# Half B of a recurrent step: which product is made from bf16 parts, how its x term arrives, and how the x work is dealt out over eight steps

## The chip, the cores and the metric

The kernel runs on one core of one Trainium2 chip. The metric is the device time of one execution in microseconds (us). Before the change it is 1639.37 us, the median of three runs (1638.94 to 1640.77).

## The reference

A gated recurrence runs over 512 time steps for a batch of 8, with 512 inputs and 512 hidden units, everything in float32:

```python
fused = jax.nn.sigmoid(jnp.concatenate([x_t, h], axis=-1) @ w_W + w_b)
hidden_state, output_state = jnp.split(fused, 2, axis=-1)
memory_state = x_t @ wx_W + wx_b + hidden_state * (h @ wh_W + wh_b)
h_new = output_state * h + (1.0 - output_state) * jnp.tanh(memory_state)
```

The output is x plus the stacked h_new. In the kernel's names r is the pre-activation of hidden_state, z that of output_state, and hh is h @ wh_W + wh_b. All products with x can be made ahead of time; the products with h can't, since step i+1 needs h of step i.

## The kernel before

**Layout.** The hidden units are cut into half A and half B. TensorE holds h of four chunks of 128 units (k = 0 to 3; chunks 0 and 1 come out of half A, 2 and 3 out of half B) as the stationary operand, 32 columns wide, and streams weights past it; four column tiles j of 32 columns work side by side. Four steps make a group, and a group's x terms (bias included) are spread into the PSUM banks ahead of the h products, in rows of 8 batches for each step of the group.

**A step on TensorE** follows the string `ORDER`: bank A (192 columns: hh, z and r of half A) for the four chunks, bank B (128 columns: r and hh of half B), then bank C (64 columns: z of half B, in the PSUM tile `cs`), then `x_step`, a share of the x products for a later pair of groups. A0 and B0 stand first, since chunk 0 of the new h is there first; A2 and A3 need half B of the new h.

**Bank C is made in two ways.** In float32 every product is one instruction in the program, two loads and two matmuls in the trace. From step 24 on, in every second group (steps 0 to 3 of eight, `in_parts`), it is made from bf16 parts: POOL splits h into three bf16 parts (`split`), and for each chunk and column tile one load of 24 columns (3 parts x 8 batches) serves three matmuls with three bf16 parts of the weights (`wb`, `w2`, `w3`; `kept` is a matmul that keeps the loaded operand). The three row groups of the result are added by a VectorE reduction (`tzs<-tzB`).

**The chain of a step.** VectorE transposes r, hh and z of half A out of bank A, ScalarE takes the sigmoid of r, a scan on VectorE makes r * hh + x (slots of two elements, `md0`, `md1`), ScalarE takes the tanh, and another scan makes the new h (`hT<-hd0A,hT`). It is done in two pieces for each half (`memory(hf, q)`, `update(hf, q)`). Half B follows in the same way from banks B and C.

**The x work.** `x_step` deals 2688 columns over eight steps u = 0 to 7 by the table `SHARE`. The sums end up in the SBUF tiles `even` and `odd` (even and odd groups), half by ScalarE copies and half by VectorE additions: `even[HI, XC]` is written at the end of step u = 5, `odd[LO, XC]` at the end of u = 7. `spread` copies them into banks A and B, `spread_c` into the four cells of `cs` with a mask for each step (in the other groups bank C is one copy), and `turn_x` transposes the columns of wx into `md1`.

**Queues.** The program is one list of operations in the order in which they are written; each engine takes its own in that order, and a planner puts in the waits. PSUM is guarded by bank: an access waits for the last access of any other engine to that bank. SyncE (SP) issues the loads of x (one of 64 KB at u = 1 and u = 5) and the stores of the output (one at the end of u = 3 and of u = 7).

## Time and profile before

| | us |
|---|---|
| median of three runs | 1639.37 |
| the profiled execution: its own time | 1637.59 |
| the profiled execution: span of its core | 1635.5 |
| TensorE matmul busy | 1625.4 (99%) |
| TensorE loads busy | 1397.4 (85%) |
| ScalarE busy | 1254.0 (77%) |
| VectorE busy | 1235.8 (76%) |
| GpSimd (POOL) busy | 531.8 (33%) |

The granted TensorE clock is 1.0 throughout. A busy matmul row isn't an engine at its peak, since matmuls overlap in the trace; what a step costs is read from the distance between the starts of its first matmul and that of the next step. In the rows PE is a matmul, PEld a load of the stationary operand, DVE VectorE, ACT ScalarE and SPq SyncE's DMA queue. The columns of a timeline are start (us from the span's start), length, engine, line, operation, output<-inputs, shape and count, and in brackets the idle time before it with its releaser. Nearly all rows have line 255, that of a helper that emits the program.

### The profile page before, as it was taken

To read this page: it belongs to the slowest core of one execution; us is meant where nothing else is said; L and a number is where in the kernel's file an instruction comes from. 1 tells how busy PE (TensorE), PEld (TensorE's weight loads), DVE (VectorE), ACT (ScalarE), POOL (GpSimd) and SP (SyncE) were. 2 spreads that over 40 slices of the span, in tenths; PEclk is the share of its full clock that TensorE was granted. 3 is DMA by queue.
4 is the path that set the end of the run, shared out by engine and by line. 5 is a ranking of instruction groups with operands and counts; after the bars stand their busy time and mean duration, and the time that the engine had idled before them with its cause. 6 is when DMAs were issued, how large, how long until landed. Compare 5 with 4: busy or idle time off the path is not lost.

```text
span 1635.5 us, 127307 instructions
## 1 busy us (share of the span) xinstructions
PE 1625.4 (99%) x58202; PEld 1397.4 (85%) x50394; DVE 1235.8 (76%) x9433; ACT 1254.0 (77%) x6188; POOL 531.8 (33%) x2272
## 2 busy tenths in 40 slices
PE   8999999999999999999999999999999999999998
PEld 5988898988888888888888888888888888988887
DVE  7777777777777777777777777777777777777776
ACT  4777777778777777777777777777777777777775
POOL 1323323333233333332333333323333333333332
PEclk9999999999999999999999999999999999999999
DMA  4000000000000000000000000000000000000000
GB/s 185 12 14 18 15 15 14 18 15 14 15 18 15 15 14 18 15 15 15 17 15 15 15 18 14 15 15 18 14 15 15 17 15 15 15 18 10 10 10 11
DMA packets 37297, 31.25 MB, mean 19 GB/s; under 512 B 4084, under 2 KB 35060, under 8 KB 36600
## 3 DMA queue, kind: packets, MB, share of 16 engines
q1 hardware_dynamic: 36576, 22.89, 4.5%
q8 instruction: 425, 6.96, 1.7%
q14 instruction: 144, 1.18, 0.2%
q10 hardware_dynamic: 152, 0.22, 0.0%
HBM read 14.70 MB, written 8.39 MB: 14 GB/s over the span
## 4 chain that ended last, share of the span: by engine, by line
PE 98%; DVE 1%; DMA 0%; ACT 0%; issue 0%; DVEq 0%; ACTq 0%; SPq 0%
PE A L255 41%; PE B L255 27%; PE xp L255 17%; PE cs L255 9%; PE cs L219 4%; PE eps L255 1%; DMA head<-in_xh_dram 0%; DVE tr L255 0%; DVE m L255 0%; DVE tw L255 0%; DVE hT L255 0%; DVE md1A L255 0%; DVE tz L255 0%; DVE md1B L255 0%; DVE even L255 0%
## 5 line engine op out<-in xcount | busy, mean ns | idle before, releaser
L255 PE MATMUL A<-wa,hT 128*32 128x192 f32 x16384 | 872.3, 327 | 3.2 <-DVE hT L255 3.1
L255 PEld LDWEIGHTS A<-wa,hT 128*32 128x32 f32 x16384 | 549.4, 122 | 189.8 <-DVE hT L255 132.1
L255 PE MATMUL B<-wb,hT 128*32 128x128 f32 x16384 | 652.0, 273 | 0.0
L255 PEld LDWEIGHTS B<-wb,hT 128*32 128x32 f32 x16384 | 542.5, 122 | 19.9 <-DMA wb<-in_wb_dram 0.3
L255 POOL TENSOR_TENSOR ot<-xin,hT 128x16 f32<-128x16 f32 x991 | 224.1, 250 | 598.8 <-DVE hT L255 596.8
L255 ACT ACTIVATE hT<-m 128x8 f32<-128x8 f32 x2048 | 349.2, 208 | 65.0 <-DVE m L255 64.1
L255 DVE STREAM_TRANSPOSE tr<-A 128x64 f32<-128x64 f32 x512 | 127.9, 250 | 291.9 <-PE A L255 285.8
L255 PE MATMUL xp<-tw,sx 128*32 128x384 f32 (+2 forms) x1464 | 264.0, 433 | 0.0
L255 POOL TENSOR_TENSOR split<-hT 128x32 f32<-128x32 f32 x488 | 126.0, 258 | 410.0 <-DVE m L255 397.9
L255 ACT ACTIVATE hT<-hT 128x16 f32<-128x16 f32 x1022 | 210.3, 225 | 50.1 <-DVE hT L255 47.8
L255 ACT ACTIVATE md0A<-tr 128x16 f32<-128x16 f32 x512 | 112.2, 219 | 165.4 <-DVE tr L255 158.8
L255 DVE TENSOR_TENSOR_SCAN hT<-hd0B,hT 128x24 f32<-128x24 f32 x1024 | 179.5, 204 | 75.7 <-ACT hT L255 52.4
L255 PE MATMUL xp<-wx,xin 128*32 128x384 f32 (+4 forms) x1348 | 218.3, 413 | 0.0
L255 DVE TENSOR_TENSOR_SCAN hT<-hd0A,hT 128x24 f32<-128x24 f32 x1024 | 198.3, 194 | 0.0
L255 PE MATMUL cs<-wb,hT 128*32 128x64 f32 x8576 | 173.0, 219 | 0.0
L255 PEld LDWEIGHTS cs<-wb,hT 128*32 128x32 f32 x8576 | 161.4, 122 | 0.0
L255 DVE TENSOR_TENSOR_SCAN m<-md0A,md1A 128x16 f32<-128x16 f32 x1024 | 142.3, 181 | 6.9
L255 DVE TENSOR_TENSOR_SCAN m<-md0B,md1B 128x16 f32<-128x16 f32 x1024 | 145.0, 163 | 0.6 <-issue 0.4
L255 ACT ACTIVATE hd0A<-tz 128x16 f32<-128x16 f32 x512 | 116.0, 227 | 20.9
L219 PE MATMUL cs<-w,split 128*24 128x64 bf16 x7808 | 129.9, 192 | 0.0
L255 PE MATMUL cs<-wb,split 128*24 128x64 bf16 x3904 | 122.2, 192 | 0.0
L255 POOL TENSOR_TENSOR split<-split 128x16 f32<-128x16 f32 x488 | 105.2, 216 | 38.2
(101 smaller groups left out, 2216.0 us busy)
## 6 DMA issues: line engine op xcount, KB each, us to landing
out_dram<-ot SPq DMA_DIRECT2D x128, 64.0 KB, 1.6
xin<-in_x_dram SPq DMA_DIRECT2D x112, 64.0 KB, 2.4
wx<-in_wx_dram SPq DMA_DIRECT2D x4, 768.0 KB, 7.5
wa<-in_wa_dram SPq DMA_DIRECT2D x4, 384.0 KB, 10.1
wb<-in_wb_dram SPq DMA_DIRECT2D x1, 1152.0 KB, 13.4
xin<-in_x_dram SPq DMA_DIRECT2D x3, 256.0 KB, 3.1
wb<-in_wb_dram SPq DMA_DIRECT2D x1, 384.0 KB, 13.8
head<-in_xh_dram ACTq DMA_DIRECT2D x1, 208.0 KB, 5.6
```

The costliest lines, as they stand in the source:

```text
L219: return t.add_instruction(mybir.InstMatmult(name=self.nc.get_next_instruction_name(), ins=[t.lower_ap(rhs), t.lower_ap(lhsT)], outs=[t.lo ...
L255: inst = getattr(self, item.op, getattr(engine, item.op, None))(*item.args, **item.kw)
```

## The change

1. **What is made from parts.** The third product of half B is now hh (`H` in `ORDER`) in place of z; r and z of half B come from bank B. It is made from bf16 parts in every step from 24 on (`in_parts`), into one of eight cells of `cs`. Before step 24 the same cells are filled in float32.
2. **Slots of four rows.** `split` has four rows for each batch: three parts and a row of zeros. So the 32 rows of a column tile in a cell are 8 batches x 4. The fourth row of the cell holds the x term, the first one the bias of hh. A scan over four elements for each batch (`md0B` holds 0 or 1, 1, 1, r; `memB` is the transposed cell) adds the three parts, multiplies by r and adds the x term, so the reduction and half B's `turn_x` go.
3. **The x term travels by DMA.** `move_x` issues 16 DMAs for each group, of 8 partitions x 64 columns each, from `even` or `odd` into the fourth rows of `xz`, one for each step of the group and each column tile. `fill` copies one step of `xz` into its cell on ScalarE, two steps ahead, in every step; `spread_c` and the copies into bank C go.
4. **Shares of the x work.** `SHARE` becomes 306, 384, 384, 384, 308, 306, 308, 308 for u = 0 to 7 (it was 384 four times and 288 four times). The sum stays 2688.
5. POOL splits h in every step from 24 on, not in half of them; before that it copies h into the split tile.

The core of the diff:

```diff
-ORDER = "A0 B0 A1 A2 A3 B1 B2 B3 C0 C1 C2 C3"
+ORDER = "A0 B0 A1 A2 A3 B1 B2 B3 H0 H1 H2 H3"
...
-SHARE = [384, 384, 384, 384, 288, 288, 288, 288]
+SHARE = [306, 384, 384, 384, 308, 306, 308, 308]
...
-XP = {"A": slice(0, 192), "X": slice(192, 320), "C": slice(320, 384), "B": slice(384, 512)}
+XP = {"A": slice(0, 192), "X": slice(192, 256), "M": slice(256, 320), "B": slice(320, 448)}
...
+    def products_h(i, k):
+
+        four = split[i % 2]
+        for j in range(NQ):
+            to = cell(i)[32 * j : 32 * j + 32]
+            if not in_parts(i):
+                mm(to, four[:, k].rearrange("p b u -> p (b u)"), wh("H", k, j))
+                continue
+            lhsT = high(four)[:, k].rearrange("p b u -> p (b u)")[:, 1::2]
+            for n, t_ in enumerate((wh("H", k, j), w2[:, k, j], w3[:, k, j])):
+                (nc.tensor.kept if n else mm)(to, lhsT, high(t_)[:, 1::2])
...
     def in_parts(i):
-        return 3 * NH <= i < T and i // GS % 2 == 0
+        return 3 * NH <= i < T
...
+    def move_x(g):
+
+        at = (even, odd)[g % 2]
+        if source(g) is not at:
+            nc.scalar.copy(at[:, XP["M"]], source(g)[:, XP["M"]])
+        for s in range(GS):
+            for j in range(NQ):
+                r = 32 * j
+                (nc.sync if g or s else nc.scalar).dma_start(
+                    out=xz[g % 2][r + 3 : r + 32 : 4, s],
+                    in_=at[r + B * s : r + B * s + B, XP["M"]],
+                )
+
+    def fill(i):
+        if i < T:
+            nc.scalar.copy(cell(i), xz[i // GS % 2][:, i % GS])
...
-            "h": (pa[:, :HU], ps["B"][:, HU:]),
-            "z": (pa[:, HU : 2 * HU], cell(i)),
-            "r": (pa[:, 2 * HU :], ps["B"][:, :HU]),
+            "h": (pa[:, :HU], cell(i)),
+            "z": (pa[:, HU : 2 * HU], ps["B"][:, :HU]),
+            "r": (pa[:, 2 * HU :], ps["B"][:, HU:]),
...
-            scan(c_, ms[hf], md0[hf][g % 2][:, rows], md1[hf][g % 2][:, rows])
-            act(state(hf, i, 1)[:, :, c_], ms[hf][:, :, c_, 1], AF.Tanh)
+            d1 = memB.rearrange("p c (n s) -> p n c s", s=4) if hf else md1[g % 2][:, rows]
+            scan(c_, ms[hf], md0[hf][g % 2][:, rows], d1)
+            act(state(hf, i, 1)[:, :, c_], ms[hf][:, :, c_, SL[hf] - 1], AF.Tanh)
...
         turn_r(1)
+        turn_z(1)
+        update(0, 0)
         turn_h(1)
-        update(0, 0)
...
+        for n in (1, 2) if i == 0 else () if i == T - 6 else (i + 1, i + 2) if i == T - 5 else (i + 2,):
+            fill(n)
...
         elif u == 5:
             if sums:
                 nc.vector.tensor_tensor(even[HI, XC], reg(BE), both[HI], ALU.add)
+            if sums or o + 1 == LAST:
+                move_x(2 * o + 2)
...
             if o:
                 nc.scalar.copy(odd[LO, XC], reg(GA))
-            turn_x(2 * o + 2, 1)
+            if sums:
+                move_x(2 * o + 3)
```

How the change moves instructions is shown on three engines. First VectorE, from the transposes of half B to the last update in a step that was made from parts before (`tr` is r, `md1B` hh, `tzB` the three row groups of z, `m` the scan of the memory state, `hT` the new h). Before:

```order
L255 STREAM_TRANSPOSE tr_1_136<-B_117 128x64 [waits flow_tensor]
L255 STREAM_TRANSPOSE md1B_86<-B_117 128x64
L255 SCALAR_TENSOR_TENSOR hT_69<-hd0A_89,hT_68 128x24 [waits flow_scalar]
L255 STREAM_TRANSPOSE tzB_156<-cs 128x64 [waits flow_tensor]
L255 SCALAR_TENSOR_TENSOR m_1_133<-md0B_82,md1B_86 128x16 [waits flow_vector,flow_scalar]
L255 TENSOR_REDUCE tzs_157<-tzB_156 128x16 [waits flow_vector]
L255 SCALAR_TENSOR_TENSOR hT_69<-hd0A_89,hT_68 128x24
L255 SCALAR_TENSOR_TENSOR m_1_133<-md0B_82,md1B_86 128x16
L255 SCALAR_TENSOR_TENSOR hT_69<-hd0B_91,hT_68 128x24 [waits flow_scalar] x2
```

The same place after the change, in a step u = 5 (`memB` is the transposed cell of hh):

```order
L257 STREAM_TRANSPOSE tr_1_138<-B_119 128x64 [waits flow_tensor]
L257 STREAM_TRANSPOSE tz_1_139<-B_119 128x64
L257 SCALAR_TENSOR_TENSOR hT_73<-hd0A_89,hT_72 128x24 [waits flow_scalar]
L257 STREAM_TRANSPOSE memB_133<-cs 128x64 [waits flow_tensor]
L257 SCALAR_TENSOR_TENSOR hT_73<-hd0A_89,hT_72 128x24 [waits flow_scalar]
L257 SCALAR_TENSOR_TENSOR m_1_135<-md0B_85,memB_133 128x32 [waits flow_vector]
L257 SCALAR_TENSOR_TENSOR m_1_135<-md0B_85,memB_133 128x32
L257 SCALAR_TENSOR_TENSOR hT_73<-hd0B_91,hT_72 128x24 [waits flow_scalar] x2
```

The reduction is gone, the scans of half B take 32 elements, and the first of them waits for VectorE's own transpose of the cell, two instructions ahead of it. The first update of half A stands at the same place.

Second ScalarE, from the last tanh of a step u = 6 to the first sigmoid of the next step (`cs<-...` fills a cell, `hT<-hT` copies the new h into another slot, A and B are banks). Before:

```order
L255 ACTIVATE hT_73<-m_2_140 128x8 [waits flow_vector] x2
L255 ACTIVATE cs<-even,mask 128x64 x2
L255 ACTIVATE hT_74<-hT_74 128x8x2
L255 ACTIVATE hT_74<-hT_74 128x8x2 [waits flow_vector]
L255 COPY A_116<-even 128x192
L255 COPY B_117<-even 128x128
L255 ACTIVATE md0A_81<-tr_3_148 128x2x8 [waits flow_vector]
```

After:

```order
L257 ACTIVATE hT_73<-m_2_143 128x8 [waits flow_vector] x2
L257 COPY cs<-xz_80 128x64 [waits flow_dma13,flow_dma14,flow_dma12,flow_dma11]
L257 ACTIVATE hT_74<-hT_74 128x8x2
L257 ACTIVATE hT_74<-hT_74 128x8x2 [waits flow_vector]
L257 COPY A_116<-even 128x192
L257 COPY B_117<-even 128x128
L257 ACTIVATE md0A_83<-tr_3_152 128x2x8 [waits flow_vector]
```

One copy stands where two masked copies stood, and it waits for four DMAs. A copy like it now stands in every step.

Third SyncE's queue. Before, eight steps hold two stores and two loads in turn, and only the stores wait (for POOL's sums). After, from a store at the end of u = 3 to the next store at the end of u = 7:

```order
L257 DMA out_dram<-ot_158 128x128 [waits flow_gpsimd]
L257 DMA xin_132<-in_x_dram 128x128
L257 DMA xz_80<-even 8x64 x2
L257 DMA xz_80<-even 8x64 [waits flow_vector]
L257 DMA xz_80<-even 8x64 x13
L257 DMA xz_81<-odd 8x64 [waits flow_scalar]
L257 DMA xz_81<-odd 8x64 x3
L257 DMA xz_81<-odd 8x64 [waits flow_dma19]
L257 DMA xz_81<-odd 8x64 [waits flow_dma20]
L257 DMA xz_81<-odd 8x64 [waits flow_dma21]
L257 DMA xz_81<-odd 8x64 [waits flow_dma22]
L257 DMA xz_81<-odd 8x64 x8
```

There are 32 more DMAs in eight steps, between one store and the next. The first two of the even group read partitions that ScalarE wrote at u = 2; the third waits for the VectorE addition of u = 5.

177 lines of the change are left out of this document (83 added, 94 removed).

## The prediction

> **What bounds the kernel now.** I read the page's busy times and its chain that ended last, then the waits, then the timeline of TensorE over two kinds of steps. A change of less than 0.2% (3.3 us) is what a measurement of this kernel can't tell from no change.
>
> ```profile
> PE 1625.4 (99%) x58202; PEld 1397.4 (85%) x50394; DVE 1235.8 (76%) x9433; ACT 1254.0 (77%) x6188; POOL 531.8 (33%) x2272
> PE 98%; DVE 1%; DMA 0%; ACT 0%; issue 0%; DVEq 0%; ACTq 0%; SPq 0%
> PEld A L255 <- DVE hT L255: 132.1, 402, 0.8
> PE A L255 <- DVE hT L255: 3.1, 9, 0.6
> ```
>
> Matmuls make 98% of the chain, and TensorE waits for the new h only 9 times. But the load for bank A waits for it 402 times, so the loop through h ends just ahead of the matmuls. How far ahead is read step by step:
>
> ```profile
> 797.64 0.52 PE L255 MATMUL A<-wa,hT 128*32 128x192 f32 x8
> ...
> 799.82 0.64 PE L255 MATMUL cs<-wb,hT 128*32 128x64 f32 x32
> 800.26 0.42 PE L255 MATMUL xp<-wx,xin 128*32 128x288 f32 x2
> ...
> 800.68 0.22 PEld L255 LDWEIGHTS A<-wa,hT 128*32 128x32 f32 x8 [0.28 <-DVE hT L255]
> ...
> 800.75 0.52 PE L255 MATMUL A<-wa,hT 128*32 128x192 f32 x8
> ...
> 802.92 0.21 PE L255 MATMUL cs<-wb,split 128*24 128x64 bf16 x3
> ...
> 803.28 0.49 PE L255 MATMUL xp<-wx,xin 128*32 128x384 f32 x2
> ...
> 803.93 0.52 PE L255 MATMUL A<-wa,hT 128*32 128x192 f32 x8
> ```
>
> The first step has u = 7, with bank C in float32: banks A and B 2.18 us, C 0.44, x 0.49 for 288 columns, in all 3.11. The next has u = 0: 2.17, 0.36 from parts, 0.65 for 384 columns, in all 3.18. Eight steps take 4 x 3.11 + 4 x 3.18 = 25.16 us. In the first, the load is released 0.07 us ahead of its matmul, and the next rows show what happens without x work, where nothing hides the loop:
>
> ```profile
> 21.80 0.55 PE L255 MATMUL A<-wa,hT 128*32 128x192 f32 x8 [0.62 <-DVE hT L255]
> 24.88 0.55 PE L255 MATMUL A<-wa,hT 128*32 128x192 f32 x8 [0.24 <-DVE hT L255]
> ```
>
> Here TensorE idles 0.24 us in a step, and the step still takes 3.08 us. That is the **floor of the loop**: bank A, transposes, sigmoid, scan, tanh, scan, A0 of the next step. Float32 steps stand only 0.03 above it, steps from parts 0.10.
>
> **The change on TensorE.** hh of half B from parts in all steps takes 0.44 - 0.36 = 0.08 us out of each float32 step. The x work is only dealt out anew (2688 columns both times): 306 or 308 columns take 0.49 x 307 / 288 = 0.52, 384 take 0.65. The loads now have 32 columns in bf16, not 24.
>
> ```profile
> L255 PEld LDWEIGHTS cs<-wb,split 128*24 128x24 bf16 x3904 | 107.4, 93 | 9.9
> L255 PEld LDWEIGHTS cs<-wb,hT 128*32 128x32 f32 x8576 | 161.4, 122 | 0.0
> ```
>
> The last number of a row's name is its count, then busy us and mean ns. The trace has no bf16 load of 32 columns. It may cost nothing more (the matmuls cover it), or as much as the float32 one: 29 ns for each of four chunks, 0.12 us. I take 0.01, so 0.37 for the stage, since the 24-column stage with 16 loads already fits into 0.36. The Trainium skill, page "TensorE: Matmul & The Clock Gate", section "LDWEIGHTS (loading the stationary operand)", speaks against this part: a load's time goes by its columns, about P / 1.2 ns, so 8 more columns would be 6.7 ns; by it, four column tiles side by side would add 0.03 us to a step (an estimate), and the sum below would rise by some 3 us. No run here shows it.
>
> So three steps need 2.17 + 0.37 + 0.65 = 3.19 us of matmuls, and five need 2.17 + 0.37 + 0.52 = **3.06, which is less than the floor of 3.08**. The x work that leaves them doesn't shorten them to 3.06; the loop is late next. That is the main step of this prediction.
>
> **Does the floor move?** Half A's part of the loop keeps its instructions and their order up to `update(0, 0)`; one transpose of half B stands where another stood. Half B gets its hh last, and it then passes a scan, a tanh and a scan:
>
> ```profile
> 797.45 0.23 DVE L255 STREAM_TRANSPOSE tz<-cs 128x64 f32<-128x64 f32 x1
> ...
> 797.68 0.25 DVE L255 TENSOR_TENSOR_SCAN m<-md0B,md1B 128x16 f32<-128x16 f32 x2
> ...
> 798.13 0.31 DVE L255 TENSOR_TENSOR_SCAN hT<-hd0B,hT 128x24 f32<-128x24 f32 x2 [0.20 <-ACT hT L255]
> ...
> 798.19 1.17 PE L255 MATMUL A<-wa,hT 128*32 128x192 f32 x24
> ```
>
> The scan of the memory state starts at 797.68, just as the transpose of `cs` ends, and it will be the same transpose, now of hh, that it needs. So half B comes as in float32 steps, but for two terms. The new wait of that scan for the transpose's end: the rows show no such wait; with a gap of 0 now I put it at 0.03, with 0 and the 0.07 that a load keeps to its matmul (800.68 to 800.75) as bounds. And the scans have 32 elements.
>
> ```profile
> L255 DVE TENSOR_TENSOR_SCAN m<-md0B,md1B 128x16 f32<-128x16 f32 x1024 | 145.0, 163 | 0.6 <-issue 0.4 <-DVE tzB L255 0.2
> L255 DVE TENSOR_TENSOR_SCAN m<-md0A,md1A 128x16 f32<-128x16 f32 x1024 | 142.3, 181 | 6.9
> L255 DVE TENSOR_TENSOR_SCAN hT<-hd0A,hT 128x24 f32<-128x24 f32 x1024 | 198.3, 194 | 0.0
> L255 DVE TENSOR_TENSOR_SCAN hT<-hd0B,hT 128x24 f32<-128x24 f32 x1024 | 179.5, 204 | 75.7 <-ACT hT L255 52.4
> L255 DVE TENSOR_REDUCE tzs<-tzB 128x16 f32<-128x64 f32 x244 | 66.1, 271 | 0.0
> ```
>
> Eight more elements cost 13 to 41 ns by these rows (194 - 181, 204 - 163), of which the larger holds a wait; sixteen I put at 0.02, with bounds 0.02 and 0.08. A2 is the second third of the group at 798.19 (1.17 us, the last 0.2 of it one matmul running out, so 0.32 a chunk) and starts at about 798.52; the first update of half B ends near 798.13 + 0.20 = 798.33. The load takes some 0.05 to see it (an estimate) and 0.07 to its matmul. So 0.07 is spare, less the 0.02 to 0.03 by which A0 comes sooner at the floor, against 0.05 added: it fits or misses by a hair, and I put the floor at **3.09**. The reduction that goes (271 ns) stood in steps whose loop had 0.10 to spare, so by itself it brings nothing, but those steps now share the 3.09 floor: only u = 0 of them has the shorter x share.
>
> **POOL and ScalarE.** POOL splits in twice as many steps: four instructions, 0.95 us a step by the first two rows. It is busy 33% now, some 14 points more then, and no wait of TensorE for a split is among the waits of the steps that have it, so I cost it at nothing; uncovered it would be one more split, 0.2 us a step. ScalarE gets a fill of 216 ns in every step and loses masked copies of 303 (four in eight steps) and one copy of 216:
>
> ```profile
> L255 POOL TENSOR_TENSOR split<-hT 128x32 f32<-128x32 f32 x488 | 126.0, 258 | 410.0 <-DVE m L255 397.9
> L255 POOL TENSOR_TENSOR split<-split 128x16 f32<-128x16 f32 x488 | 105.2, 216 | 38.2
> ...
> L255 ACT ACTIVATE cs<-even,mask 128x64 f32<-128x64 f32 x252 | 68.6, 303 | 1.6
> L255 ACT COPY cs<-odd 128x64 f32<-128x64 f32 x63 | 13.6, 216 | 1.5
> ...
> 805.62 0.48 ACT L255 COPY both<-xp 64x384 f32<-64x384 f32 x1
> ...
> 806.00 0.22 ACT L255 ACTIVATE md0A<-tr 128x16 f32<-128x16 f32 x1
> ```
>
> That is 8 x 216 against 4 x 303 + 216, or 0.3 us more in eight steps. The tightest step is u = 0, whose two long copies end at 806.10, as the next sigmoid starts. There half B's tanh comes about 0.2 earlier without the reduction, which pays for the fill: 0, with a bound of 0.1 us once in eight steps (6 us in all).
>
> **The 32 DMAs.** No DMA between SBUF tiles is in this trace; the nearest rows:
>
> ```profile
> out_dram<-ot SPq DMA_DIRECT2D x128, 64.0 KB, 1.6
> xin<-in_x_dram SPq DMA_DIRECT2D x112, 64.0 KB, 2.4
> ```
>
> ```profile
> 789.83 0.33 SPq L255 DMA_DIRECT2D out_dram<-ot  x1
> 790.21 0.43 SPq L255 DMA_DIRECT2D xin<-in_x_dram  x1
> ...
> 803.28 1.08 SPq L255 DMA_DIRECT2D xin<-in_x_dram  x1
> ```
>
> ```profile
> 795.35 0.56 DVE L255 TENSOR_TENSOR even<-xp,both 64x384 f32<-64x384 f32 x1
> ...
> 798.23 0.55 ACT L255 ACTIVATE cs<-even,mask 128x64 f32<-128x64 f32 x2
> 798.72 0.34 ACT L255 ACTIVATE hT<-hT 128x16 f32<-128x16 f32 x2
> ...
> 799.70 0.22 ACT L255 ACTIVATE md0A<-tr 128x16 f32<-128x16 f32 x1 [0.23 <-DVE tr L255]
> ```
>
> At 0.38 to 0.43 us an issue, 36 DMAs take SyncE about 15 of 25 us: it keeps up. The narrow place is the even group: the addition of u = 5 ends at 795.91, and the fill of u = 6 is due at 798.23, so 2.3 us later. The first two of the four DMAs it waits for read what ScalarE wrote at u = 2 and go out ahead. The other two are issued at about 795.96 and 796.36; at 1.6 to 2.4 us they land at 797.96 to 798.76. Behind the fill stand the two slot copies, the spread into A and B, and the next sigmoid: ScalarE has been idle for 0.23 at 799.70, so the copies take from 798.72 to 799.47. A fill at 798.76 ends at 798.98, the copies 0.75 later, at 799.73, against 799.70 - 0.03. I take 1.6 (an SBUF source, the smaller rows): **0**. The other DMAs have a step or more.
>
> **The sum.** With 59 periods of eight steps from step 24 on: 5 x 3.09 + 3 x 3.19 = 25.02, so 0.14 less a period, 8.3 us. At the edges: the steps before 24 gain on one share what they lose on the others; in the last group `move_x` comes one step ahead of two fills, whose eight DMAs need 8 x 0.41 + 1.6, so near 5 us against some 2.3 + 1.3 of room: 1 to 2 us once, less about half a microsecond in the last steps from parts. I take +1. The profiled execution (1637.59, its span 1635.5 and 2.1 around it) would become 1630.3; the median of the runs is 1.8 above that execution, so **1632 us**.
>
> **Rivals.**
> 1. *The floor isn't there* (TensorE sets all steps, because A0's load slips behind the x matmuls at no cost): 5 x 3.06 + 3 x 3.19 = 24.87, 17 us less, 1623. For it speaks that TensorE waits 9 times only; against it the 3.08 of steps with nothing else to do. 0.20.
> 2. *Half B becomes the loop's end*: if its added terms pass the 0.05 that fits by 0.03, A2 waits and five steps take 3.12; 25.17, no gain, 1640. The spare time is a difference of small numbers. 0.18.
> 3. *The fill of u = 6 is late* (slower): it decides once a DMA takes over 2.4 us from issue to landing. Then ScalarE stands at the fill, with the slot copies, the spreads and the next sigmoid behind it, and every 0.1 us costs 59 x 0.1 = 6 us. At 2.9 us that is 30 - 7, so 1662; with the SyncE issue of 1.08 us it is reached at 1.8 us of landing. The Trainium skill, page "DMA: Bandwidth & Descriptors", section "Rules for kernel authors", says to join many small transfers into a large one, since below 64 KB one pays mostly overhead; these have 2 KB, so it speaks for this rival. The median rows don't. 0.14.
> 4. *The 32-column loads aren't covered*: the 0.01 lies between bounds of 0 and 0.12. At 0.05 the sum is 5 x 3.10 + 3 x 3.23 = 25.19, so 1642; from there on the gain is gone, and at 0.12 (25.75) it would be 1675. 0.06.
> 5. That the order of the bf16 products isn't what the change says is ruled out: TensorE's list has one load and three matmuls for each tile in every step from 24 on.
>
> **How the numbers follow.** My forecast has 0.42. Faster: 0.42 + 0.20 = 0.62. Within 0.2%: rival 2 and half of rival 4, 0.21. Slower: rival 3 and the other half, 0.17. The range takes in rival 1 and rival 2 whole with ScalarE's bound on top, and leaves out most of rival 3: 1621 to 1647.
>
> **What would show it.** Starts of bank A 3.08 to 3.10 us apart in five steps of eight, with the load released by `hT<-hd0A,hT` and the matmul 0.02 to 0.06 behind it, and 3.19 in three, say the floor is right; 3.06 says rival 1. A wait in front of A2 named `hT<-hd0B,hT` says rival 2. Idle time of ScalarE in front of `cs<-xz` with a DMA as releaser says rival 3. The stage from parts at 0.36 to 0.38 us answers rival 4. Steps that are longer though no such wait stands in them would make the whole account wrong.

## The result, and the profile after

The changed kernel took **1930.18 us** (median of 6 runs, 1920.82 to 1935.04), the kernel before 1639.03 on the same chip (6 runs, 1638.0 to 1640.77): a ratio of 1.1772, 95% interval 1.1743 to 1.1802. The forecast was 1632. The kernel is 291 us slower; no end of the range comes near it.

First the page after, its span, busy times and the chain that ended last by engine:

```profile
span 1933.3 us, 132353 instructions
...
PE 1743.1 (90%) x62594; PEld 1366.0 (71%) x46978; DVE 1226.5 (63%) x9063; ACT 1233.8 (64%) x6382; POOL 774.8 (40%) x3296
...
PE 38%; SPq 33%; DVE 11%; DMA 10%; ACT 5%; issue 4%; DVEq 0%; POOL 0%; ACTq 0%
```

TensorE made 98% of the chain before and makes 38% now. SyncE's issuing of DMAs (SPq) and the DMAs themselves stand in its place. The waits name who stood behind them (us in total, times, longest):

```profile
DVE odd L257 <- DMA xz<-odd: 210.6, 61, 5.0
PEld xp L257 <- DVE odd L257: 144.3, 60, 3.9
PE xp L257 <- DVE odd L257: 133.4, 60, 3.7
ACT cs L257 <- DMA xz<-even: 35.0, 55, 2.4
```

About once in each eight steps VectorE waits 3.5 us before it may write `odd`, and TensorE's x products wait for that addition. One round of it in the timeline (start, length, then engine, line and operation, with the idle time ahead in brackets):

```profile
962.20 0.55 DVE L257 TENSOR_TENSOR odd<-xp,both 64x384 f32<-64x384 f32 x1 [2.20 <-DMA xz<-odd]
963.77 15.43 SPq L257 DMA_DIRECT2D xz<-even  x16
968.25 0.56 DVE L257 TENSOR_TENSOR even<-xp,both 64x384 f32<-64x384 f32 x1
979.24 10.63 SPq L257 DMA_DIRECT2D xz<-odd  x16
...
991.14 0.55 DVE L257 TENSOR_TENSOR odd<-xp,both 64x384 f32<-64x384 f32 x1 [3.59 <-DMA xz<-odd]
991.74 0.55 PE L257 MATMUL xp<-tw,xin 128*32 128x308 f32 x2 [2.34 <-DVE odd L257]
```

This is a circle. Two of the 16 even transfers go out early; the other 14 wait for the even addition, which ends at 968.81. From then on SyncE issues without a pause: 14 for even, 16 for odd, until 989.87. That is 21.06 us for 30 issues, **0.70 us each**. The next addition into `odd` overwrites what the odd transfers read, so it waits for the last of them, and starts at 991.14. TensorE's x products wait for it, and all that follows, the next even addition too, is late by as much. The window holds 28.9 us from one odd addition to the next; eight steps took 25.16 before. Over steps 32 to 479 the mean is 29.98.

In most rounds a second loss follows the wait. The granted TensorE clock is 1.0 in the rows above, but 48 times in this trace it stands at 0.5 for up to 3.4 us (165 us of 1933, mean clock 0.958), and 46 of these stretches begin 0.8 to 2.7 us after the start of an odd addition. The 45 rounds with such a stretch take 30.5 us in the median, the 13 without it 28.7. The step u = 5 takes 4.2 to 4.8 us with it and 3.2 without. So some 80 us of the 291 (an estimate, 45 x 1.8) come from the lower clock behind the wait. The runs below in which the odd addition doesn't wait for its transfers have no such stretch between steps 32 and 479, save e4, whose fills wait instead.

Four groups of the page answer to smaller terms of the forecast (busy us, mean ns of one, idle ahead):

```profile
L257 POOL TENSOR_TENSOR split<-hT 128x32 f32<-128x32 f32 x976 | 254.9, 261 | 1011.0 <-DVE hT L257 1003.0
...
L257 PEld LDWEIGHTS cs<-wb,split 128*32 128x32 bf16 (+1 forms) x8576 | 222.9, 97 | 35.0 <-ACT cs L257 5.9
L257 DVE TENSOR_TENSOR_SCAN hT<-hd0B,hT 128x24 f32<-128x24 f32 x1024 | 185.1, 220 | 86.6 <-ACT hT L257 86.6
...
L257 DVE TENSOR_TENSOR_SCAN m<-md0B,memB 128x32 f32<-128x32 f32 x1024 | 173.5, 211 | 0.0
```

The loads of 32 columns take 97 ns in this row, or 96 without the 768 float32 loads that it also holds; those of 24 took 93. Half B's memory scan has 211 against 163, and its update 220 against 204 although it still has 24 elements. That last number is looked into below.

### The profile page after: what moved, and what is told of

Same layout as the page of the kernel before. It is cut to its first block, busy times and chain, and to the rows that moved or that the text cites. A ratio compares the mean times of both kernels' runs of the same rounds, so it can differ in the third digit from the quotient of the medians.

```text
span 1933.3 us, 132353 instructions
## 1 busy us (share of the span) xinstructions
PE 1743.1 (90%) x62594; PEld 1366.0 (71%) x46978; DVE 1226.5 (63%) x9063; ACT 1233.8 (64%) x6382; POOL 774.8 (40%) x3296
## 4 chain that ended last, share of the span: by engine, by line
PE 38%; SPq 33%; DVE 11%; DMA 10%; ACT 5%; issue 4%; DVEq 0%; POOL 0%; ACTq 0%
SPq L257 33%; PE A L257 21%; PE B L257 9%; DMA xz<-odd 6%; PE xp L257 4%; DMA xz<-even 3%; DVE m L257 2%; DVE tr L257 2%; PE cs L221 2%; ACT hT L257 2%; DVE odd L257 2%; DVE tz L257 2%; ACT xp L257 1%; PE cs L257 1%; DVE hT L257 1%
## 5 line engine op out<-in xcount | busy, mean ns | idle before, releaser
L257 PE MATMUL A<-wa,hT 128*32 128x192 f32 x16384 | 948.7, 347 | 42.0 <-DVE hT L257 41.5
L257 POOL TENSOR_TENSOR split<-hT 128x32 f32<-128x32 f32 x976 | 254.9, 261 | 1011.0 <-DVE hT L257 1003.0
L257 PE MATMUL cs<-wb,split 128*32 128x64 bf16 (+1 forms) x8576 | 258.8, 195 | 6.8 <-ACT cs L257 3.8
L257 PE MATMUL xp<-tw,sx 128*32 128x384 f32 (+4 forms) x1708 | 262.4, 395 | 0.0
L221 PE MATMUL cs<-w,split 128*32 128x64 bf16 x15616 | 258.2, 192 | 0.1
L257 POOL TENSOR_TENSOR split<-split 128x16 f32<-128x16 f32 x976 | 222.7, 228 | 76.4
L257 PEld LDWEIGHTS cs<-wb,split 128*32 128x32 bf16 (+1 forms) x8576 | 222.9, 97 | 35.0 <-ACT cs L257 5.9
L257 PE MATMUL xp<-tw,xin 128*32 128x308 f32 x976 | 112.8, 330 | 133.4 <-DVE odd L257 133.4
L257 PE MATMUL xp<-wx,xin 128*32 128x384 f32 (+6 forms) x1592 | 219.6, 375 | 0.2 <-ACT xp L257 0.2
L257 DVE TENSOR_TENSOR_SCAN m<-md0B,memB 128x32 f32<-128x32 f32 x1024 | 173.5, 211 | 0.0
```

The source lines that it names most:

```text
L221: return t.add_instruction(mybir.InstMatmult(name=self.nc.get_next_instruction_name(), ins=[t.lower_ap(rhs), t.lower_ap(lhsT)], outs=[t.lo ...
L257: inst = getattr(self, item.op, getattr(engine, item.op, None))(*item.args, **item.kw)
```

## The experiments

Three accounts were set against each other. Theory 1: SyncE's row of issues, and who waits for its end. Theory 2: the steps themselves became longer. Theory 3: the traffic of many small transfers disturbs other engines. Ratios are to the kernel before on the same chip, with 95% intervals. "Eight steps" is the sum, over u = 0 to 7, of the median distance between first matmuls, steps 32 to 479. "Waits on issue" sums the rows of the waits in which TensorE's matmuls or loads stood idle and nothing in the profile released them; a late load and its late matmul are both in it.

| run | ratio | eight steps, us | waits on issue, us |
|---|---|---|---|
| before (e9: the same again) | 1 | 25.16 (25.17) | 8.6 (12.0) |
| after | 1.1772 | 30.12 | 14.3 |
| e1 no moves (e12: again) | 1.0142 (1.014) | 25.37 | 28.9 (21.7) |
| e2 two odd tiles | 1.0379 | 25.60 | 52.0 |
| e3 before, with idle transfers | 1.009 | - | 31.9 |
| e4 halves sent at once | 1.1368 | - | 17.6 |
| e5 no moves, split held | 1.0129 | 25.26 | 29.4 |
| e6 no moves, 16-element scan | 1.0092 | 25.15 | 31.1 |
| e7 through DRAM (e13: again) | 1.0238 (1.024) | 25.42 | 21.8 (31.5) |
| e8 through DRAM, split held | 1.0192 | 25.28 | 30.6 |
| e10 two odd tiles, fill one ahead | 1.0499 | 25.59 | 75.5 |
| e11 e7 with four edits | 1.0277 | 25.30 | 69.2 |
| e14 e11 with the old shares | 1.0191 | 25.14 | 40.5 |
| e15 e10, one line moved | 1.0348 | 25.63 | 71.4 |
| e16 e7, one line moved | 1.0188 | 25.40 | 29.5 |
| e17 e14, one line moved | 1.0145 | 25.34 | 49.9 |

### What the transfers cost

**e1, no moves** (half B's x term left out from group 2 on):

```diff
-        for s in range(GS):
+        for s in range(GS if g < 2 else 0):
             for j in range(NQ):
```

> The changed kernel without the DMAs of move_x from the third group on, so that the fills copy old x terms (the x term of half B's memory state is left out). Theory 1, SyncE's queue: a DMA of 8 partitions takes 0.667 us from issue to issue, and the addition into odd at u = 3 waits for the last of 30 of them; without them eight steps fall from 30 to about 25.0 us and the time to 1622 to 1640. Theory 2, the steps themselves (scans of 32 elements, a fill and splits in every step) have become longer: the time stays above 1800. Theory 3, the many small packets disturb the other engines' reads and writes: 1622 to 1640 as in theory 1.

1669.38 us against 1646.7, 1.0142 (1.0112 to 1.0171). That is above the 1622 to 1640 of theories 1 and 3 and far below the 1800 of theory 2. The transfers make all but 1.4 points of the 17.7%. The rest is no matter of transfers and stays a loss: without any of them the change is slower.

**e2, two odd tiles in turn**, so that the odd addition has a tile that no transfer reads:

```diff
-        at = (even, odd)[g % 2]
+        at = odds[g // 2 % 2] if g % 2 else even
...
-                nc.vector.tensor_tensor(odd[HI, XC], reg(GA), both[LO], ALU.add)
+                nc.vector.tensor_tensor(odds[(o + 1) % 2][HI, XC], reg(GA), both[LO], ALU.add)
```

> All DMAs stay; two tiles odd in turn, so that the addition at u = 3 writes a tile whose DMAs were issued a period earlier. Theory 1: no wait is left in the addition, SyncE needs 32 x 0.667 + 4 x 0.45 = 23.2 us in eight steps of about 25, so the time falls to 1630 to 1670, the upper end if fills of the even group still wait for its DMAs. Theory 2 and theory 3: same instructions and same traffic, so it stays above 1850.

1.0379 (1.0355 to 1.0404): with the same 36 issues in eight steps, 1708 us where there were 1930, though not the 1630 to 1670 expected. So the greater part is not the traffic, and not the issuing as such, but the addition that waits for the end of the row. In the waits the rival named ahead takes its place, the late fill:

```profile
ACT cs L257 <- DMA xz<-even: 39.9, 59, 2.6
```

**e3, the kernel before with 16 idle transfers at every u = 5**, in five shapes, 80 steps each. Nobody reads what they write.

```diff
+        if form and i % 8 == 5:
+            for n in range(16):
+                nc.sync.dma_start(out=scratch[form[1], n], in_=bias[form[0], 256:320])
```

> The kernel before with 16 idle DMAs at each u = 5, between SBUF tiles that nobody waits for, of another form in each stretch of 80 steps: 8 partitions to every fourth one, 8 to 8 in a row, 16 to 16, 32 to every fourth, 128 to 128. Theory 1: the issue spacing of the 8-partition forms is 0.667 us, that of 128 partitions about 0.43 as for the loads of x, and the time stays within 1636 to 1645, since SyncE has room and nobody waits. If the cost lies in the stride, the second form is cheap; if it lies in using fewer than 16 DMA engines, the third is cheap. Theory 3: steps are longer in the stretches with the DMAs.

Its timeline, SyncE's queue, 8 partitions to 8 above and 128 to 128 below:

```profile
547.58 9.19 SPq L255 DMA_DIRECT2D scratch<-bias  x13
557.37 0.33 SPq L255 DMA_DIRECT2D out_dram<-ot  x1
557.75 0.43 SPq L255 DMA_DIRECT2D xin<-in_x_dram  x1
...
1312.60 9.47 SPq L255 DMA_DIRECT2D scratch<-bias  x13
```

Thirteen issues in 9.19 and 9.47 us, where the store and the load that stand alone have 0.33 and 0.43. From one issue to the next the median is 0.72 us with 8 partitions and 0.63 to 0.65 with 16 to 128, where 0.43 had been expected for 128. (Single ones take 1.4 us and more, so that a row of 16 has 0.69 to 0.80 each on the mean.) So the price belongs to a transfer between SBUF tiles on this queue, large or small, and not to the 8 partitions. The run had 1661.2 us against 1646.7, a single time and above the 1636 to 1645 expected; the steps' medians hardly moved, and TensorE's waits on issue rose to 31.9.

**e4, each half of a tile sent as soon as it is written**, with four `xz` tiles:

```diff
                 nc.scalar.copy(even[LO, XC], reg(AL))
+                move_x(2 * o + 2, (0, 1))
...
-                move_x(2 * o + 2)
+                move_x(2 * o + 2, (2, 3))
```

> All DMAs stay, but each half of even and odd is sent as soon as it is written: even's lower half at u = 2, odd's upper half at u = 3, even's upper half at u = 5, odd's lower half at u = 7, with four tiles xz. Theory 1: the addition into odd no longer waits, and the fill of u = 6 has two DMAs ahead of it, not the whole group: 1628 to 1650. Theory 2 and 3: above 1850.

A miss: 1873.8 us, 1.1368 (1.1324 to 1.1412). Its timeline:

```profile
935.10 5.34 SPq L257 DMA_DIRECT2D xz<-even  x8
940.48 5.29 SPq L257 DMA_DIRECT2D xz<-odd  x8
943.85 0.56 DVE L257 TENSOR_TENSOR even<-xp,both 64x384 f32<-64x384 f32 x1
946.78 5.33 SPq L257 DMA_DIRECT2D xz<-even  x8
949.24 0.22 ACT L257 COPY cs<-xz 128x64 f32<-128x64 f32 x1 [2.52 <-DMA xz<-even]
...
ACT cs L257 <- DMA xz<-even: 211.4, 64, 4.9
```

The even addition ends at 944.41, but its transfers go out at 946.78, since eight odd ones, which nobody needs for five steps or more, stand in the queue ahead of them. The fill then waits 2.52 us, with the next step's sigmoid behind it on ScalarE. The last row, from the list of waits, has the sum: the wait has moved from the odd addition to the fills, and with it come 31 stretches at a clock of 0.5. To issue earlier in a queue taken in order is to put the urgent behind the early.

**e7, five transfers a group instead of 16**, through a scratch tensor in DRAM, and the fill one step ahead of its use instead of two:

```diff
+        there = nc.sync.dma_start(out=moved[g % 2], in_=at[:, XP["M"]])
...
         for s in range(GS):
...
+            read = nc.sync.dma_start(
+                out=xz[g % 2][3:128:4, s],
+                in_=moved[g % 2].rearrange("(j q) c -> j q c", j=NQ)[:, B * s : B * s + B],
+            )
+            nc.after(read, there)
...
-        for n in (1, 2) if i == 0 else () if i == T - 6 else (i + 1, i + 2) if i == T - 5 else (i + 2,):
-            fill(n)
+        fill(i + 1)
```

> The changed kernel, with each group's 16 small transfers replaced by five: one of 128 rows to a scratch tensor in DRAM, and four back, one for each step; the fill is made one step ahead instead of two, so that it is not late. All terms are computed. Theory 1, the 291 us are SyncE's row of 30 issues at 0.67 us between one addition into the odd tile and the next: SyncE has 14 issues in eight steps instead of 36, the wait of the odd addition on its transfers (210.6 us) goes, and the time is that of the run without moves within 10 us: 1662 to 1682 us. If it is the landing of transfers as such, or their traffic beside the other engines: 1700 us or more, since as many bytes are moved twice.

1.0238 (1.022 to 1.0255), and 1680.7 us in the repeat (e13, 1.024). SyncE's queue in the timeline of e16, which differs by one line:

```profile
607.22 0.32 SPq L257 DMA_DIRECT2D moved<-even  x1
610.01 2.19 SPq L257 DMA_DIRECT2D xz<-moved  x4
```

Five issues, with the wait for the first to land between them, are over 5 us after they begin. The Trainium skill, page "DMA: Bandwidth & Descriptors", section "Rules for kernel authors", says to join many small transfers into one. By that rule the trace agrees: with twice the bytes in 5 transfers instead of 16, e16 takes 13.5% less time than the changed kernel (1.1772 to 1.0188). Most of this is the wait of the odd addition, which also goes in e2. Against e15 below, which has the 16 transfers and no such wait, it is 1.5%.

**e10, two odd tiles with the fill one step ahead**, and **e15, e16**, which mend a line. In the runs with the fill one step ahead (e7, e8, e10, e11, e13, e14) group 2's transfers stood ahead of the fill of step 3. So step 3 took half B's x term from group 2, and waited for its transfers, once: 21.6 us for that step in e10, 8.5 in e7, 3.5 without. The edit of e15 to e17:

```diff
                 keep(2)
-                move_x(2)
         elif u == 2:
+            if o == 0:
+                move_x(2)
```

> The changed kernel with its 32 transfers in eight steps as they are, two odd tiles in turn, and the fill made one step ahead instead of two. All terms are computed. With two odd tiles alone the time was 1708 us (3.8% over before), and ScalarE waited 39.9 us for the even transfers with the fill of the step two ahead. Theory 1, SyncE's row decides only through who waits for its end: the odd addition no longer does, the fill now has a step more, and 36 issues at 0.67 us and less, some 24 us, just fit into eight steps of 25.4: the waits go, and the time is 1.5 to 2.8% over before, 1664 to 1687 us at 1640, like the run through DRAM. If SyncE's row is too long for eight steps, it falls behind by itself and the fill or the additions wait again: 1695 us or more.

> The run with two odd tiles and the fill one step ahead, with one line moved: group 2's transfers are issued a step later, after the fill of step 3. In the four runs with the fill one step ahead so far they stood ahead of that fill, so that step 3 took half B's x term from group 2, and waited for its transfers: step 3 lasted 21.6 us there, 3.5 without. All terms are right now. The wait at step 3 goes, 18 us; the steps' medians (25.59 in eight) and TensorE's waits on issue stay: 3.4 to 4.2% over before, where the one before it had 5.0.

> The run with five transfers a group through DRAM, with the same line moved. All terms are right. Step 3 lasted 8.5 us and falls to about 3.5: 1.8 to 2.2% over before, where the first one had 2.4. What then remains against the kernel before is half B's late chain (25.42 against 25.17 in eight steps, some 15 us) and TensorE's waits on issue (some 10 to 20 us).

e10 missed, with 1.0499; e15 has 1.0348 (1.0333 to 1.0364), e16 1.0188 (1.0174 to 1.0203), both as expected. The repeated wait of ScalarE for even transfers is gone with the fill one step ahead, so SyncE's row does fit into eight steps. What e15 still has over e16 goes mostly with the last column of the table: 71 us of waits on issue against 30.

### What the steps themselves lost

In e1 four of the five short steps take 3.16 to 3.18 us (u = 0: 3.155, u = 5 to 7: 3.166 to 3.178); u = 4, after three long ones, takes 3.058. Each step that follows a short one loses about 0.11 us: 0.03 between A0 and B0, 0.045 in front of A2 (A1 to A2 0.37 us, 0.325 otherwise) and 0.04 in front of A3. The long step u = 1 follows a short one and loses as much: 3.29 where the other long steps have 3.18. So in eight steps five losses, 0.55 us, stand against the 0.32 that the shorter steps save. The timeline of e1 shows how half B comes:

```profile
602.73 0.22 DVE L257 STREAM_TRANSPOSE memB<-cs 128x64 f32<-128x64 f32 x1
...
602.99 0.34 DVE L257 TENSOR_TENSOR_SCAN m<-md0B,memB 128x32 f32<-128x32 f32 x2
...
603.48 0.22 POOL L257 TENSOR_TENSOR split<-split 128x16 f32<-128x16 f32 x1
...
603.49 0.36 DVE L257 TENSOR_TENSOR_SCAN hT<-hd0B,hT 128x24 f32<-128x24 f32 x2 [0.17 <-ACT hT L257]
...
603.81 0.19 PEld L257 LDWEIGHTS A<-wa,hT 128*32 128x32 f32 x8 [0.22 <-DVE hT L257]
```

By medians, counted from the start of the last bank A matmul: the memory scan starts at 1.78 us (1.75 in the float32 steps before), 0.03 after the end of its transpose. Its first piece takes 224 ns (166 before). The first update takes 268 (208 before). The load for A2 is released at 2.61 (2.46 before): 0.15 later, of which 0.03 is the start, 0.06 the longer scan, and 0.06 an update that has no more to do than before. GpSimd's second subtraction lies on it from 603.48 to 603.70. In u = 1, where that subtraction is the one that takes longer (276 ns, not 225), the update has 209.

**e5, half A's split held until half B's first update** (half B's x term left out, as in e1):

```diff
+            if hf == 0:
+                nc.after(sub.ins, first_b)
```

> The run without the moves, and in addition GpSimd holds half A's split until the first update of half B has run. The x term of half B is left out. In the run without the moves (1669.4 us) the first update of half B took 268 ns in seven of eight steps while GpSimd's second subtraction of half A's split (2280 to 2505 ns on the step's clock) lay on it (2290 to 2557), and 209 in the one step in which that subtraction was the longer of the two (276); TensorE waited in front of A2 in the five steps that follow a short one. Theory A, the split of half A collides with half B's update: the update takes 205 to 210 ns in every step, A1 to A2 falls from 368 to 310 to 330 ns, the five steps from 3.16 to about 3.11, and the time to 1650 to 1657 us. Theory B, half B is late because its memory scan can only start once the H stage is read, and the overlap costs nothing: the time stays at 1666 to 1672 us. Against both: GpSimd is now late with the split, and TensorE waits in front of the H stage; then over 1675.

1.0129 (1.0114 to 1.0144), not to be told from e1, though the mechanism is there: the update has 208 ns in every step and A1 to A2 is 0.325. The collision went elsewhere. GpSimd's additions for the output now lie on half A's memory scan in the steps with a difference of x:

```profile
603.64 0.46 POOL L257 TENSOR_TENSOR ot<-xin,hT 128x16 f32<-128x16 f32 x2
...
603.80 0.33 DVE L257 TENSOR_TENSOR_SCAN m<-md0A,md1A 128x16 f32<-128x16 f32 x2
```

The same two scans take 0.28 in e1 (602.13). In these four steps (u = 0, 1, 4, 5) half A's update comes 70 ns later. In the others a rest of half B's delay stays: the load for A2 is released at 2.55 to 2.57 us (2.61 in e1, 2.46 before), and A2 to A3 takes 0.35 us in the steps behind a short one (0.36 in e1). So the short steps have 3.12 to 3.14. **e8**, the same edit on e7:

> Both edits together: five transfers a group through DRAM with the fill one step ahead, and half A's split held until half B's first update. All terms are computed. If the transfers' issues and the collision are the two causes, the losses add up and are gone together: 1648 to 1660 us, about as long as the kernel before on the same chip; under 1640 would show that the forecast's floor of 3.09 us a step is reached. Over 1680 if a wait behind the transfers stays.

1.0192 (1.0177 to 1.0207) against 1.0238 for e7 beside it: half a per cent, less than expected.

**e6, the memory scan with 16 elements** (two of hh's three parts and the x term of half B left out):

```diff
-            d1 = memB.rearrange("p c (n s) -> p n c s", s=4) if hf else md1[g % 2][:, rows]
+            d1 = memB.rearrange("p c (n s) -> p n c s", s=4)[:, :, :, ::2] if hf else md1[g % 2][:, rows]
```

> The run without the moves, with half B's memory scan over 16 elements instead of 32: two of the four slots, and with them the two smaller parts of hh and the x term of half B, are left out. If the length of the scan is what makes half B late, the first scan takes 166 to 170 ns as before the change instead of 224, A2 is released about 55 ns sooner, and the time falls from 1669.4 to 1650 to 1658 us. If GpSimd's overlap with the update is what counts, the update stays at 268 ns or falls by itself, as it moves against the subtraction, and the scan's length alone brings under 5 us. If the late start (1780 ns on the step's clock instead of 1752) is the whole of it, nothing changes: 1666 to 1672.

1656.4 us, inside the expectation, though on a quicker chip: 1.0092 (1.0077 to 1.0107) is 0.5% under e1, where 0.7 to 1.2 had been expected. The scan has 180 ns on the page's mean (212 in e1), its first piece 192 (224 in e1, 166 to 170 expected). The wait in front of A2 is nearly gone, and eight steps take 25.15 instead of 25.37: 0.22 us, 13 us in 59 periods. But this is not the scan's length alone. The update now starts some 0.035 us sooner, and GpSimd's subtraction is mostly the one that takes longer (272 ns), so that the update has 208 to 210 ns in six steps of eight, in e1 in one. Two rows tell the terms apart. Behind u = 4 and u = 7 of e6, where the update still has 266 to 269 ns, A1 to A2 is 0.33 us. In e14 (below) the scan is as long as in e1, the update has 208 ns in every step, and A1 to A2 is 0.325. So either of the two nearly ends the wait in front of A2.

### What was left

e1, e6 and e7 are slower in time than their medians say: the mean of eight steps in e1 is 25.66, the sum of medians 25.37. Single steps are 0.3 to 0.9 us longer. There TensorE waits on issue. e9, e12, e13 and e14 ask where that comes from.

> The kernel before, unchanged, for its trace on the chip of the following runs. In the runs without moves, with the held split and through DRAM, TensorE stands idle with no releaser in the profile (its waits on issue) for 22 to 30 us in all, in the first profile of the kernel before for 9 us. If these idle times are the chip's or the execution's, this trace shows 20 us or more of them at a time of about 1645; if they belong to the changed code, it shows 6 to 12 at about 1640.

> The run without the moves once more, for its trace beside the two that follow (the x term of half B is left out). TensorE's waits on issue, its idle time that nothing else in the profile ends, were 8.6 and 12.0 us in the two traces of the kernel before, 28.9 here without any move, 31.9 in the kernel before with idle transfers, and 52.0 and 75.5 in the two runs with two odd tiles. If they come from the changed code's matmuls alone, 25 to 33 us here on any chip; if the chip or the execution sets them, anywhere from 10 to 70.

> The changed kernel with five transfers a group through DRAM, once more. It had 21.8 us of TensorE's waits on issue, the version built on it 69.2, on another chip. If these waits go with the code and its transfers, 18 to 30 us here; if the chip sets them, about as many as in the run after this one, whatever that shows.

e9 had 12.0 us at 1642.23, e12 21.7 at 1664.37, e13 31.5 at 1680.73. Neither e12 nor e13 lies where it was expected (25 to 33 and 18 to 30), and two traces of the same code differ by 7 and by 10 us; so the chip or the execution sets a part of that size. Beyond it the changed code has 22 to 32 us without the moves or through DRAM (e11, e14 and e17, which differ in more, have 40 to 69), against 9 to 12 in the kernel before. Runs with small transfers have more (e3 31.9; e2, e10 and e15 52 to 75), save where TensorE stands still for another reason (after 14.3, e4 17.6). Rows of the waits, the kernel before, then e15:

```profile
PEld xp L255 <- issue: 5.1, 21, 0.8
```

```profile
PEld cs L257 <- issue: 25.2, 56, 0.9
PEld xp L257 <- issue: 19.1, 57, 0.8
```

**e11** joins what the runs had shown; **e14** and **e17** take its shares back, e17 with the line of e15.

```diff
+            sub = nc.gpsimd.tensor_tensor(t_[:, :, :, 2], t_[:, :, :, 0], high(t_)[:, :, :, 1], ALU.subtract)
+            if hf == 0:
+                nc.after(sub.ins, first_b)
...
-        nc.gpsimd.tensor_tensor(t_[n], a, b, op)
+        nc.vector.tensor_tensor(t_[n], a, b, op)
...
-SHARE = [306, 384, 384, 384, 308, 306, 308, 308]
+SHARE = [320, 384, 384, 320, 320, 320, 320, 320]
-EARLY = 76
+EARLY = 128
```

`EARLY` shifts where the dealing begins and goes with the shares.

> A version from what the runs showed, with all terms: five transfers a group through DRAM (the first and the last group as in the changed kernel), the fill one step ahead; of half A's split only the second subtraction held until half B's first update; the four differences of x a group moved from GpSimd to VectorE, so that GpSimd's additions for the output end before VectorE's memory scan; columns 384 in two steps and 320 in six. If GpSimd's overlap with VectorE is what lengthened the short steps, the update of half B takes 210 ns, no scan over 235 ns is left in front of it, six steps take 3.10 to 3.13 us and two 3.18 to 3.22, 25.0 to 25.2 in eight steps against 25.16 before: 1628 to 1648 us at 1640 for the kernel before, no measurable difference or a small gain. If half B is late for its longer scans and its late start alone, the short steps stay at 3.15 and the time at 1655 or more.

> The last version with the changed kernel's dealing of the columns, 384 in three steps and 306 to 308 in five, in place of 384 in two and 320 in six: the other edits stay. If the dealing of columns, which cuts each eight steps' matmuls and loads into 1736 instead of 1720, sets how often TensorE runs out of instructions, its waits on issue fall from 69 to 20 to 32 us and the time is 0 to 1% over before. If the held subtraction and VectorE's differences do it, or the quicker steps as such, they stay at 55 to 80 us and the time at 2 to 3% over before.

> The run with the changed kernel's shares and GpSimd's work moved out of VectorE's way, with the same line moved. All terms are right. Step 3 lasted 9.3 us and falls to about 3.5: 1.3 to 1.7% over before, where the last one had 1.9. Eight steps' medians, 25.14, are then those of the kernel before, and what is left over is TensorE's waits on issue, 30 to 45 us against 9 to 12.

In the steps e11 and e14 did what was hoped: the update has 208 ns, A1 to A2 0.325, and most short steps 3.07 to 3.14 us; e14's eight steps, 25.14, are those of the kernel before by their medians. By their mean they are 25.60 against 25.19, since single steps are long, those of u = 0 above all (3.04 to 3.88 us). e11 had 69 us of waits on issue, and e14 40, between what its two accounts expected. The times are 1.0277 (a miss), 1.0191 and, without the wait at step 3, 1.0145 (1.0123 to 1.0167) for e17. That time is within its expectation; e17's waits, 49.9 us, and its eight steps, 25.34 (u = 0 has 3.28), are above it. No version beat the kernel before. Why e11 had 69 and e7 22 is open; the shares account for a part of it only.

## Why the prediction was wrong

**The step that failed: "At 0.38 to 0.43 us an issue, 36 DMAs take SyncE about 15 of 25 us: it keeps up" and "The other DMAs have a step or more".** The price in the first and the check in the second both failed, and mending one of them alone would not have saved the forecast. The price came from the nearest rows, single transfers between DRAM and SBUF. Transfers between SBUF tiles issued in a row took 0.67 to 0.70 (after) and 0.63 to 0.72 (e3). And the end of the row was checked for one reader only, the fill of u = 6. The last 16 transfers read `odd`, which VectorE writes at u = 3. In e1 the even addition ends at 604.45 and the odd one starts at 624.00, so the row has 19.5 us. By my price 30 issues and a landing are 30 x 0.41 + 1.6 = 13.9, which fits; by the measured one 30 x 0.70 + 1.3 = 22.3, which doesn't. The forecast asked how soon the data must *arrive* and not until when its source must be *kept*. By the measured price alone, 36 issues still fit into eight steps, as e15 shows. e2, where the source is kept, takes 222 us off; e16 takes 256 off. Some 80 of these (the estimate above) are the clock of 0.5 that follows the wait, for which the forecast had no term.

**Rival 3, the late fill of u = 6,** is real and was not the bound: 35.0 us of waits after, 39.9 in e2. e15's fill one step ahead removes them, and the ratio falls only from 1.0379 to 1.0348. It was priced by landing time, while in e4 the queue ahead of the transfers made it late.

**Rival 2, half B becomes the loop's end,** is true too, and is what e1 shows: "A2 waits". It was priced at 3.12 us for five steps; four of them took 3.16 to 3.18 and one, u = 4, 3.06, and the long step u = 1 took 3.29, since the loss falls on the step behind a short one. The terms: the self-wait, put at 0.03, was 0.03. The scan of 32 elements, put at 0.02 with bounds 0.02 and 0.08, was 0.06. GpSimd's split, **costed at nothing**, was 0.06, not as a wait for the split but as time in which it and VectorE get in each other's way (in e5, with the split held, the update has 208 ns). 0.05 was forecast, 0.15 came. The working asked who waits for GpSimd, and not what runs beside it. The Trainium skill, page "GPSIMD Engine Reference", section "1. Specifications", says that GpSimd's access to SBUF is shared with VectorE and contended by VectorE instructions with two SBUF inputs, as a scan is. By that rule the split was not free; the trace agrees, 268 ns against 208.

**The floor of 3.08 to 3.09** is near what single steps have where half B is less late: 3.078, 3.084 and 3.098 in u = 4, 6 and 7 of e6, 3.074 in u = 4 of e14. No run has it in all five short steps. u = 4 of e1 takes 3.058, less than the floor, and the step behind it then has B0 0.354 us after A0 in place of 0.325; from B0 to B0 that is 3.087. Rival 1 (3.06 in all five) fell. That the loop is late where TensorE needs less than it was right, and the long steps had 3.18 to 3.19 where nothing waited, in e1 in u = 2 and 3.

**Rival 4** fell: the stage from parts takes 0.36 us with loads of 32 columns, as with 24. The Trainium skill, page "TensorE: Matmul & The Clock Gate", section "LDWEIGHTS (loading the stationary operand)", has a load's time go by its columns. By that rule the forecast had an estimate of 0.03 us more a step, and the trace doesn't show it. **ScalarE's fill** at 0 was right where its data are there: in e1 half A's first scan starts 0.915 to 0.942 us after the last bank A matmul, before the change 0.916 to 0.932.

**Not on the list:** TensorE's waits on issue. e16, with all terms and the transfers out of the way, is 30 us slower than before: (25.40 - 25.17) x 59 = 14 us for half B, and 29.5 - 12.0 = 17.5 us more of these waits. (The waits count a late load and its late matmul both, so 17.5 may be too much; by how far the mean of eight steps lies above their medians, 0.31 us in e16 and 0.03 to 0.10 before, an estimate is 12 to 17.) The forecast had a gain of 8.3 us in the steps, which these two terms outweigh even without the transfers.

## What to carry to other kernels

A transfer out of a buffer binds its writer as well as its reader: for every DMA that is added, ask who next writes its source, and sum the issues that stand in the queue ahead of it at the price of that kind of transfer in a row. A price for an issue taken from single transfers of another kind was off by a factor of 1.7 here, and a row of them showed it. Where TensorE is made to stop, read the granted clock behind the stop too. An engine that isn't waited for can still cost time through what runs beside it: place GpSimd's work where VectorE's chain has nothing to do.

## What was not expected of the hardware

**SyncE takes 0.63 to 0.72 us, by medians, for a transfer between SBUF tiles in a row** (e3), from 8 to 128 partitions alike (2 to 32 KB), against 0.33 to 0.43 for a single one of 64 KB to or from DRAM, 0.32 for one of 128 rows to DRAM and 0.55 each for four in a row from DRAM.

**Overlap of GpSimd and VectorE costs one of the two 50 to 80 ns, not its whole wait.** The Trainium skill, page "SBUF — State Buffer", section "SBUF: two separate sides", says that whichever engine starts first holds the shared port for its whole instruction while the other fully blocks. Here an update that starts 10 ns after the subtraction of 225 ns and has 208 ns to do ends after 268: less than the sum, 433. In u = 1 it starts 6 ns after, has 209, and the subtraction has 276. So by these rows what is shared is held for a part of the instruction only, and a few nanoseconds decide who pays; spans on GpSimd are rough, so the sizes are too.

**TensorE seems to run out of instructions.** The page of e1 lists the instruction queues and TensorE's instruction counts:

```profile
PE 1648.0 (99%) x62594; PEld 1348.0 (81%) x46978; DVE 1227.8 (74%) x9063; ACT 1232.3 (74%) x6382; POOL 774.5 (46%) x3296
...
q8 instruction: 430, 7.05, 1.8%
```

430 packets of 16 KB for 62594 + 46978 matmuls and loads are 255 for each packet; before the change it is 425 for 108596, or 256. In the trace of e15, 62 loads of the H stage or of x start more than 0.42 us after the start of the load ahead of them, and 60 of these start 1.2 to 1.6 us after the end of the latest such packet, although packets come every 3.9 us. That ties these waits to the supply of instructions by their times; no run changed the supply alone. Why small transfers, and some versions more than others, make it late was not settled. The Trainium skill, page "Runtime: NRT & Kernel Launch", section "Instruction fetch mechanics", calls refills in blocks of 256 instructions mostly hidden; the blocks agree, and hidden they are here nearly, and only in the kernel before.

**The granted clock halves behind a wait of TensorE.** In the changed kernel it stands at 0.5 for 3.4 us in most rounds, as said above, and the matmuls of bank A then take twice the time (A1 to A2 0.64 us in u = 5, where 0.325 is the least).
